# Layer 1 spline: the clip moved into scalar_tensor_tensor, r of every second half on VectorE, one distance instruction for a unit

## The chip, the cores and the metric

The kernel runs on one core of a Trainium2 chip. The metric is the device time of one launch in microseconds (us), the median of several runs. A core has five engines that run side by side: TensorE (PE, matmuls), VectorE (DVE, elementwise and reductions), ScalarE (ACT, functions of one input), GpSimd (POOL) and SyncE (SP, here the issue of DMA transfers). SBUF is the working memory of 128 partitions, PSUM the memory into which TensorE accumulates. Each engine takes its instructions in the order in which they were written down.

## The reference

The input x has 4 images of 16 channels and 256 x 256 pixels, float32. Two layers follow, each with a group normalization (8 groups) in front and the input added at the end:

```
x = x + L0(group_norm(x))     # a 3x3 convolution gives 25 weights a pixel and channel; softmax; weighted sum of the 5x5 patch
x = x + L1(group_norm(x))     # below
```

Layer 1 is the one that the change concerns. Its patches are 3 x 3 with padding 1:

```
bspl = b_splines(patches, grid)            # 8 cubic B-spline bases of every value, uniform grid
out  = silu(patches) . base_w  +  bspl . spl_w  +  bias
```

so that it is a 3x3 convolution over 16 x 8 spline features plus a 3x3 convolution over 16 silu features, to 16 output channels.

## The kernel before

**Layer 0** takes about the first two thirds. A chain of TensorE (logits), ScalarE (exponential), GpSimd (product) and VectorE (sum over the 25 places) runs over strips of columns. The change doesn't touch it. It writes its result x1 to DRAM.

**Layer 1** works on 64 units: 4 images, each in 16 bands of 16 rows. Its SBUF partitions are the 128 features: 16 channels x 8 spline bases. A loop over the units `n` writes down, for each:

- `features(n, put)`: the spline features of the 16 new rows of the unit, into `ring`, a buffer of 50 rows that holds three units and two rows more. The rows are worked in two halves of 8 rows (8 x 256 = 2048 elements a partition; at an image's first band one half has 9 rows, at its last 7). Between the halves, `put` (line 944) adds the bias to the finished output of the unit before the last and moves it from PSUM to SBUF.
- `silu(n, ...)`: the silu features of the unit (line 908), on ScalarE.
- `halo(n)`: zeroes at image borders; where the unit lies at the start of the ring, a DMA copies two rows from its end to its start.
- `load_x(n + 2)`: the loads of x1, two halves of 1 MB, each channel spread over eight partitions. There are three tiles, `xta`, `xtb` and `xtc`, used in turn (`xtt[n % 3]`).
- `store()` of an output, `load_tiles(n + 1)`: the tile `sx` for silu and the residual.
- `outputs(n, sx)`: 128 matmuls into `yp`: 96 on `ring` (line 961), 8 on `sx` (969), 24 on the silu features (977). All but the first two of the 96 need rows of half 1.

**The spline.** A basis is a function of the distance t of the normalized value from the basis' center, in grid steps. Up to a factor that the weights carry, it is

f = -max(2 - t, 0)^3 + 4 max(1 - t, 0)^3

For each half, ScalarE makes the distance in place in the tile of x1 (`Abs`, line 923), then r = max(1 - t, 0) (`Relu`, line 158), (2 - t)^2 into s2 (line 159) and 4 r^2 into s1 (line 160). VectorE clips t in place to min(t, 2) - 2 (line 161, a tensor_scalar), multiplies s2 by it (162) and s1 by r (163), and adds the two into `ring` (164). The temporaries r, s2 and s1 are one set for half 0 (`ta`) and one for half 1 (`tb`), with no second copy: ScalarE can fill a set for unit n+1 only when VectorE is done with it for unit n.

The order on each engine is the order of writing, for the loops above; a few units of layer 1 start while layer 0 ends, and their place among layer 0's instructions is given by marks. SyncE's issues also stand in this order: the loads of `n + 2` behind the ring copy of `n`, the sx tiles of `n + 1` behind the store of an output. `spline` is used once more at the start, for the value of the features outside the image (one element a partition).

Of the kernel before, what the change touches and what calls it, by code (L numbers as in the profile page):

```python
# [13 lines left out]
AF = mybir.ActivationFunctionType  # L14
ALU = mybir.AluOpType
# [18 lines left out]
def conv_preact_kernel(  # L34
# [12 lines left out]
    nc = tc.nc  # L47
    B, C, H, W = x.shape
# [34 lines left out]
    hs = [dram.tile([NST, HP, C, SP], F32, name=f"hs{b}") for b in range(B)]  # L83
# [68 lines left out]
        nc.gpsimd.tensor_tensor(rstd, var, mhalf, ALU.pow)  # L152
        return mean, rstd

    def spline(f, t, r1, s2, s1):


        nc.scalar.activation(r1, t, AF.Relu, bias=1.0, scale=-1.0)  # L158
        nc.scalar.activation(s2, t, AF.Square, bias=2.0, scale=-1.0)  # L159
        nc.scalar.activation(s1, r1, AF.Square, scale=2.0)  # L160
        nc.vector.tensor_scalar(t, t, 2.0, 2.0, ALU.min, ALU.subtract)  # L161
        nc.vector.tensor_mul(s2, s2, t)  # L162
        nc.vector.tensor_mul(s1, s1, r1)  # L163
        nc.vector.tensor_add(f, s2, s1)  # L164

    def scales(b, psum):

# [43 lines left out]
    sc = {}  # L211
# [177 lines left out]
    with tc.tile_pool(name="prep0", bufs=2) as prep, tc.tile_pool(  # L389
# [58 lines left out]
        nc.vector.tensor_copy(ub, ups)  # L448
        nc.scalar.activation(edge[:, 0:1], ub, AF.Abs)
        spline(*(edge[:, k : k + 1] for k in (4, 0, 1, 2, 3)))  # L450
        wps = pstat.tile([1, NL], F32, name="wps", tag="wps")

# [58 lines left out]
        for b in range(B):  # L511
            st = stat.tile([P, G, NH * (GC if b == 0 else 1), 6], F32, name=f"st0_{b}", tag=f"st0{min(b, 1)}")
            for hf in range(NH):
                n = b * NH + hf
                t = loaded.pop(0)
# [310 lines left out]
    def layer1(arm, last, marks):  # L826
# [3 lines left out]
        with ExitStack() as pools:  # L830
# [4 lines left out]
            def temps(name):  # L835
                p = pool(name)
                return [p.tile([P, RU // 2 + 1, W], F32, name=f"{name}{k}{arm}") for k in range(3)]

            def fixed(name, shape, n=1):
                p = pool(name)  # L840
                t = [p.tile(shape, F32, name=f"{name}{k}{arm}") for k in range(n)]
                return t

            XT = [P, RU + 1, W]
            xt0, tmp0 = fixed("xta", XT), temps("ta")
            sxp, yop = pool("sx", 2), pool("yo", 3)
            tmp1, xt1 = temps("tb"), fixed("xtb", XT)
            ring = fixed("ring", [P, 3 * RU + 2, W + 2])[0]
            sl, xtt = fixed("sl", [RD * C, RU // RT, W + 2], 2), xt0 + xt1 + fixed("xtc", XT)
# [13 lines left out]
            def halves(u):  # L863
                lo, hi = span(u)
                mid = (lo + hi + 1) // 2
                return lo, ((lo, mid), (mid, hi))
# [4 lines left out]
            def place(n):  # L871
                b, u = units[n]
                return (2 * (b % 2) + u) % 3 * RU
# [41 lines left out]
            def features(n, between):  # L915
                b, u = units[n]
                lo, hs = halves(u)
                r0 = place(n)
                for k, ((a, z), tmp) in enumerate(zip(hs, (tmp0, tmp1))):
                    if k == 1:  # L920
                        between()
                    xt = xtt[n % 3][:, a - lo : z - lo]
                    nc.scalar.activation(xt, xt, AF.Abs, scale=sc[b][2], bias=sc[b][3])  # L923
                    spline(
                        ring[:, r0 + a : r0 + z, 1 : W + 1], xt, *(t[:, 0 : z - a, :] for t in tmp)
                    )

            def halo(n):
                b, u = units[n]
# [70 lines left out]
            for t in sl:  # L1000
                for e in (0, W + 1):
                    nc.gpsimd.memset(t[:, :, e : e + 1], 0.0)
            features(0, put)
            first_silu = len(nc.cur_bb.bb.instructions)
            silu(0, sx[0])
            for n in range(len(units)):
                if n % 2:
                    next(more, None)
                if n > 0:
                    features(n, put)  # L1010
                    silu(n, sx[n])
                halo(n)
                if n + 2 < len(units):
                    for half in range(2):
                        load_x(n + 2, half)
                store()
                if n + 1 < len(units):
                    sx.append(load_tiles(n + 1))
                outputs(n, sx[n])
# [60 lines left out]
```

## Time and profile before

| what | value |
|---|---|
| time, median of 3 runs (lowest to highest) | 3223.17 us (3222.82 to 3223.66) |
| span of the profiled run | 3222.0 us |
| layer 1: first clip of unit 0 (L161) | starts at 2112.86 us |
| layer 1: first clip of unit 1 | starts at 2131.22 us |
| layer 1: last instruction on features (L164 of unit 63) | starts at 3199.07, takes 2.03 us |
| mean granted TensorE clock | 0.962 of full speed |

How to read the lines that follow: in the time lines, the columns are the start in us, the duration in us, the engine, the line of the kernel with operation, what is written and read, the shape (partitions x elements) and how many instructions were merged; in brackets stands how long the engine sat idle before and who released it. In the tables by stage, the columns are the stretch, its length, the busy time of PE, PEld (weight loads), DVE, ACT and POOL with instruction counts, the granted TensorE clock, the share of the DMA engines' time, and GB/s. Buffer numbers are left out of names.

### The profile page before, as it was taken

To read this page: it belongs to the slowest core of one execution; us is meant where nothing else is said; L and a number is where in the kernel's file an instruction comes from. 1 tells how busy PE (TensorE), PEld (TensorE's weight loads), DVE (VectorE), ACT (ScalarE), POOL (GpSimd) and SP (SyncE) were. 2 spreads that over 40 slices of the span, in tenths; PEclk is the share of its full clock that TensorE was granted. 3 is DMA by queue.
4 is the path that set the end of the run, shared out by engine and by line. 5 is a ranking of instruction groups with operands and counts; after the bars stand their busy time and mean duration, and the time that the engine had idled before them with its cause. 6 is when DMAs were issued, how large, how long until landed. Compare 5 with 4: busy or idle time off the path is not lost. (4 is left out here: it accounts for less than half of the span.)

```text
span 3222.0 us, 40428 instructions
## 1 busy us (share of the span) xinstructions
PE 2862.3 (89%) x14776; PEld 1490.7 (46%) x14776; DVE 3101.7 (96%) x1799; ACT 2208.0 (69%) x2233; POOL 1936.4 (60%) x659
## 2 busy tenths in 40 slices
PE   3499999999999999999999989859999989988988
PEld 3366665666566566656656656512222222222222
DVE  6589999999999999999999999999999999999997
ACT  6366555466554465554444444589999999999996
POOL 2299999999999999999999999900000000000000
PEclk7699999999999999999999999979999999999999
DMA  7988886778877788877756756678878778888883
GB/s 224 291 223 236 229 221 187 212 211 230 246 208 192 203 219 225 249 198 203 210 156 170 191 157 170 163 169 183 178 168 179 180 171 168 180 176 173 178 179 71
DMA packets 356531, 626.34 MB, mean 194 GB/s; under 512 B 45298, under 2 KB 222692, under 8 KB 340452
## 3 DMA queue, kind: packets, MB, share of 16 engines
q1 hardware_dynamic: 323300, 606.88, 75.3%
q10 hardware_dynamic: 33024, 16.78, 1.9%
q8 instruction: 121, 1.98, 0.3%
q14 instruction: 86, 0.70, 0.1%
HBM read 513.95 MB, written 104.24 MB: 192 GB/s over the span
## 5 line engine op out<-in xcount | busy, mean ns | idle before, releaser
L775 PE MATMUL lg<-wm,am 128*128 128x400 f32 x4096 | 1748.9, 508 | 123.4 <-ACT e L798 109.7
L803 POOL TENSOR_TENSOR e<-e,u 128x1600 f32<-128x1600 f32 x512 | 1789.1, 3536 | 68.5 <-ACT e L798 68.0
L680 DVE TENSOR_REDUCE nd<-e 128x128 f32<-128x3200 f32 x512 | 1747.5, 3477 | 23.3 <-POOL e L803 23.2
L798 ACT ACTIVATE e<-lg 128x800 f32<-128x800 f32 x1024 | 815.7, 836 | 896.5 <-DVE nd L680 768.9
L779 PE MATMUL lg<-wn,an 97*128 97x400 f32 x2048 | 1358.4, 663 | 0.5 <-DMA an<-hsl 0.5
L775 PEld LDWEIGHTS lg<-wm,am 128*128 128x128 f32 x4096 | 766.3, 194 | 450.1 <-ACT e L798 161.3
L961 PE MATMUL yp<-ring,wt 128*32 128x512 f32 x6144 | 755.1, 604 | 146.0 <-DVE ring L164 110.4
L779 PEld LDWEIGHTS lg<-wn,an 97*128 97x128 f32 x2048 | 390.8, 191 | 311.9 <-issue 15.6
L961 PEld LDWEIGHTS yp<-ring,wt 128*32 128x32 f32 x6144 | 206.5, 110 | 685.1 <-issue 477.9
L889 POOL MEMSET sx<- 16x256 f32 x8 | 2.4, 303 | 765.6 <-DMA out_dram<-yo 706.6
L977 PE MATMUL yp<-sl,ws 64*32 64x512 f32 x1536 | 176.5, 588 | 0.0
L164 DVE TENSOR_TENSOR ring<-ta,ta 128x2048 f32<-128x2048 f32 (+1 forms) x64 | 147.8, 2309 | 2.5
L164 DVE TENSOR_TENSOR ring<-tb,tb 128x2048 f32<-128x2048 f32 x64 | 145.6, 2276 | 2.6
L163 DVE TENSOR_TENSOR ta<-ta,ta 128x2048 f32<-128x2048 f32 (+1 forms) x64 | 147.3, 2301 | 0.0
L163 DVE TENSOR_TENSOR tb<-tb,tb 128x2048 f32<-128x2048 f32 x64 | 146.5, 2289 | 0.0
L908 ACT ACTIVATE sl<-sx,q 64x2048 f32<-64x2048 f32 x64 | 133.3, 2083 | 0.0
L160 ACT ACTIVATE ta<-ta 128x2048 f32<-128x2048 f32 (+1 forms) x64 | 122.3, 1911 | 0.0
L160 ACT ACTIVATE tb<-tb 128x2048 f32<-128x2048 f32 x64 | 120.5, 1883 | 0.6 <-POOL sx L889 0.6
L193 POOL TENSOR_TENSOR rstd<-rstd,mhalf 128x8 f32<-128x8 f32 x4 | 8.7, 2176 | 175.6 <-DVE rstd L191 175.6
L706 POOL TENSOR_TENSOR xc<-xc,nd 128x512 f32<-128x512 f32 x64 | 98.8, 1544 | 12.1 <-DVE nd L700 12.1
L977 PEld LDWEIGHTS yp<-sl,ws 64*32 64x32 f32 x1536 | 48.8, 106 | 116.2 <-issue 113.2
L923 ACT ACTIVATE xta<-xta,q 128x2048 f32<-128x2048 f32 (+2 forms) x44 | 91.6, 2083 | 0.0
(174 smaller groups left out, 2131.9 us busy)
## 6 DMA issues: line engine op xcount, KB each, us to landing
am<-hst SPq DMA_DIRECT2D x512, 194.6 KB
u<-hs SPq DMA_DIRECT2D x320, 288.0 KB
an<-hsl SPq DMA_DIRECT2D x512, 129.8 KB
xta<-x1s SPq DMA_DIRECT2D x40, 1024.0 KB
xtb<-x1s SPq DMA_DIRECT2D x40, 1024.0 KB
xtc<-x1s SPq DMA_DIRECT2D x40, 1024.0 KB
am<-hst SPq DMA_DIRECT2D x256, 129.8 KB
sx<-x1s SPq DMA_DIRECT2D x248, 128.0 KB
```

The source lines that it names most:

```text
L160: nc.scalar.activation(s1, r1, AF.Square, scale=2.0)
L163: nc.vector.tensor_mul(s1, s1, r1)
L164: nc.vector.tensor_add(f, s2, s1)
L680: nc.vector.tensor_reduce(nd[:, :, j : j + JG, :], e.rearrange("p t j m c d -> p t j c m d"), AX.XY, ALU.add,)
L706: nc.gpsimd.tensor_sub(v, v, nd[:, 1].rearrange("p j c -> p c j"))
L775: nc.tensor.matmul(lg[:, i, :NL], lhsT=am[:, o : o + P], rhs=wm.rearrange("p m c d -> p (m c d)"), start=True, stop=False,)
L779: nc.tensor.matmul(lg[:, i, :NL], lhsT=an[:, o : o + P], rhs=wn.rearrange("p m c d -> p (m c d)"), start=False, stop=True,)
L798: nc.scalar.activation(ev, lg[:, :, :NL], AF.Exp)
L803: nc.gpsimd.tensor_tensor(e[:, 1].rearrange("p j m c d -> p j (m c) d"), e[:, 0].rearrange("p j m c d -> p j (m c) d"), uv, ALU.mult,)
L908: nc.scalar.activation(sl[n % 2][:, :, 1 : W + 1], t, AF.Silu, scale=sc[b][0][0 : RD * C], bias=sc[b][1][0 : RD * C],)
L961: nc.tensor.matmul(yp[t * M : (t + 1) * M], lhsT=wt[:, d, e].rearrange("p r o -> p (r o)"), rhs=ring[:, r0 + t * RT + d : r0 + t * RT + d ...
L977: nc.tensor.matmul(yp[t * M : (t + 1) * M], lhsT=ws[:, e].rearrange("p r o -> p (r o)"), rhs=sl[n % 2][:, t : t + NT + 1 : NT, e : e + W], ...
```

## The change

Three edits to layer 1's features, meant to take work off ScalarE and VectorE:

1. **The clip goes into the two products.** Instead of min(t, 2) - 2 by an instruction of its own, s2 becomes (t - 2) (2 - t)^2 in one scalar_tensor_tensor. This is (t - 2)^3, negative inside the support and positive outside it. The last sum clips it: min(s2, 0) + s1, again one scalar_tensor_tensor.
2. **r of half 1 is made by VectorE.** `minus_r` computes min(t, 1) - 1 = -r in one tensor_scalar; with -r in place of r, s1 r comes out negative, and the last sum subtracts it. ScalarE's `Relu` remains for half 0 and for unit 0. minus_r is written ahead of both halves of its unit. Within a half, (2 - t)^2 now stands ahead of `Relu`.
3. **One distance instruction for a unit.** From unit 1 on, one `Abs` works on both halves (up to 4352 elements a partition) before anything else of the unit.

```diff
-    def spline(f, t, r1, s2, s1):
-        nc.scalar.activation(r1, t, AF.Relu, bias=1.0, scale=-1.0)
+    def minus_r(r1, t):
+        nc.vector.tensor_scalar(r1, t, 1.0, 1.0, ALU.min, ALU.subtract)
+
+    def spline(f, t, r1, s2, s1, given=False):
         nc.scalar.activation(s2, t, AF.Square, bias=2.0, scale=-1.0)
+        if not given:
+            nc.scalar.activation(r1, t, AF.Relu, bias=1.0, scale=-1.0)
         nc.scalar.activation(s1, r1, AF.Square, scale=2.0)
-        nc.vector.tensor_scalar(t, t, 2.0, 2.0, ALU.min, ALU.subtract)
-        nc.vector.tensor_mul(s2, s2, t)
+        nc.vector.scalar_tensor_tensor(s2, t, 2.0, s2, ALU.subtract, ALU.mult)
         nc.vector.tensor_mul(s1, s1, r1)
-        nc.vector.tensor_add(f, s2, s1)
+        nc.vector.scalar_tensor_tensor(
+            f, s2, 0.0, s1, ALU.min, ALU.subtract if given else ALU.add
+        )
...
-                for k, ((a, z), tmp) in enumerate(zip(hs, (tmp0, tmp1))):
+                parts = [
+                    (a, z, xtt[n % 3][:, a - lo : z - lo], [t[:, 0 : z - a, :] for t in tmp])
+                    for (a, z), tmp in zip(hs, (tmp0, tmp1))
+                ]
+
+                def distance(a, z):
+                    t = xtt[n % 3][:, a - lo : z - lo]
+                    nc.scalar.activation(t, t, AF.Abs, scale=sc[b][2], bias=sc[b][3])
+
+                if n > 0:
+                    distance(lo, hs[1][1])
+                    minus_r(parts[1][3][0], parts[1][2])
+                for k, (a, z, xt, tmp) in enumerate(parts):
+                    if n == 0:
+                        distance(a, z)
                     if k == 1:
                         between()
-                    xt = xtt[n % 3][:, a - lo : z - lo]
-                    nc.scalar.activation(xt, xt, AF.Abs, scale=sc[b][2], bias=sc[b][3])
-                    spline(
-                        ring[:, r0 + a : r0 + z, 1 : W + 1], xt, *(t[:, 0 : z - a, :] for t in tmp)
-                    )
+                    spline(ring[:, r0 + a : r0 + z, 1 : W + 1], xt, *tmp, given=n > 0 and k == 1)
```

## The prediction, made before the changed kernel ran

> **What bounds the kernel now.** I read the page's busy line first, then the busy table by stage, then the time lines of ScalarE, VectorE and TensorE through two units of layer 1, and last the DMA share unit by unit.
>
> ```profile
> PE 2862.3 (89%) x14776; PEld 1490.7 (46%) x14776; DVE 3101.7 (96%) x1799; ACT 2208.0 (69%) x2233; POOL 1936.4 (60%) x659
> ```
>
> This line would say VectorE, with ScalarE far from full. It is a mean over two layers. The changed lines run only in layer 1 (about 2110 us to the end), and there the table by stage gives, for 2300 to 3150 us, ACT 846.83 of 850 us and DVE 829.86. So both are nearly full, and the time line has to say which one waits. ScalarE through one unit, up to the start of the next:
>
> ```profile
> 2479.84 2.08 ACT L923 ACTIVATE xtb<-xtb,q 128x2048 f32<-128x2048 f32 x1
> 2481.95 1.91 ACT L158 ACTIVATE ta<-xtb 128x2048 f32<-128x2048 f32 x1
> 2483.77 1.89 ACT L159 ACTIVATE ta<-xtb 128x2048 f32<-128x2048 f32 x1
> 2485.57 1.90 ACT L160 ACTIVATE ta<-ta 128x2048 f32<-128x2048 f32 x1
> 2487.37 2.08 ACT L923 ACTIVATE xtb<-xtb,q 128x2048 f32<-128x2048 f32 x1
> 2489.48 1.91 ACT L158 ACTIVATE tb<-xtb 128x2048 f32<-128x2048 f32 x1
> 2491.30 1.90 ACT L159 ACTIVATE tb<-xtb 128x2048 f32<-128x2048 f32 x1
> 2493.10 1.90 ACT L160 ACTIVATE tb<-tb 128x2048 f32<-128x2048 f32 x1
> 2494.90 2.08 ACT L908 ACTIVATE sl<-sx,q 64x2048 f32<-64x2048 f32 x1
> 2496.89 2.08 ACT L923 ACTIVATE xtc<-xtc,q 128x2048 f32<-128x2048 f32 x1
> ```
>
> Nine instructions without a gap: 2496.89 - 2479.84 = 17.05 us a unit. VectorE, in the half unit that follows:
>
> ```profile
> 2502.75 1.23 DVE L161 TENSOR_SCALAR xtc<-xtc 128x2048 f32<-128x2048 f32 x1 [0.20 <-ACT ta L159]
> 2504.02 2.29 DVE L162 TENSOR_TENSOR ta<-ta,xtc 128x2048 f32<-128x2048 f32 x1
> 2506.22 2.29 DVE L163 TENSOR_TENSOR ta<-ta,ta 128x2048 f32<-128x2048 f32 x1
> 2508.55 2.29 DVE L164 TENSOR_TENSOR ring<-ta,ta 128x2048 f32<-128x2048 f32 x1
> 2510.76 0.74 DVE L944 TENSOR_SCALAR yo<-yp,bias_sb 128x512 f32<-128x512 f32 x1
> ```
>
> VectorE waits for ScalarE once a unit (0.2 to 0.3 us, up to 0.8). Left alone it needs 16.64 us: early in layer 1, where ScalarE is still ahead, the first multiplies of two units start at 2215.32 and 2231.96. So ScalarE's 17.05 us bounds, VectorE's 16.64 stands right behind it, and relieving ScalarE alone would bring 0.4 us a unit. TensorE waits for VectorE:
>
> ```profile
> 2536.59 10.51 PE L961 MATMUL yp<-ring,wt 128*32 128x512 f32 x94 [2.00 <-DVE ring L164]
> 2547.03 1.06 PE L969 MATMUL yp<-sx,wx 64*32 64x512 f32 x8
> 2547.91 2.76 PE L977 MATMUL yp<-sl,ws 64*32 64x512 f32 x24
> 2550.60 1.04 PE L961 MATMUL yp<-ring,wt 128*32 128x512 f32 x2
> ```
>
> From 2536.59 to 2550.60 is 14.01 us; two more matmuls cost some 0.2 of issue (94 take 10.51), so TensorE needs 14.2 us a unit. Some units have 12.2 instead of 10.5 us in the first row, nearly all behind a longer idle stretch. The DMA, in three windows of 17 us:
>
> ```profile
> 3017.00:3034.00 17.00, 14.99 (x136) 3.97 (x128) 16.54 (x10) 16.94 (x10) 0.00 (x0) 1.00 0.82 165
> 3034.00:3051.00 17.00, 14.99 (x135) 3.99 (x130) 16.54 (x10) 16.94 (x10) 0.00 (x0) 1.00 0.71 148
> 3051.00:3068.00 17.00, 15.00 (x132) 4.09 (x128) 16.54 (x10) 16.94 (x10) 0.00 (x0) 1.00 0.99 212
> ```
>
> The last two columns are the share of the DMA engines and GB/s. The mean, 175 GB/s x 17 us = 2.98 MB a unit, takes 14.0 us at the 212 GB/s seen at 0.99. It is the third resource that could take over.
>
> **What the Trainium skill says.** "VectorE: DVE Perf Modes", section "The perf-mode tier table", gives 2293 ns for a float32 tensor_tensor of 2048 elements in SBUF and 1227 for a tensor_scalar; the trace agrees (2.29 and 1.22). "ScalarE: Activation LUTs", section "What ACT_TABLE_LOAD costs", gives 0.833 ns an element and a fixed part, of which some 93 ns overlap the instruction before; here 2.08 us at 2048 and 2.29 to 2.30 at 2304 elements agree. "Vector Engine (DVE) Microarchitecture Reference", section "Points that are easy to get wrong", warns that scalar_tensor_tensor with two non-bf16 SBUF sources halves throughput, since no port is left to read the accumulator back. All four new instructions of a unit have two such sources. The trace has that operation only with one source in PSUM, beside a tensor_tensor of the same operands:
>
> ```profile
> 2091.69 0.69 DVE L699 SCALAR_TENSOR_TENSOR r<-nd,r 128x512 f32<-128x512 f32 x1
> 2092.42 0.69 DVE L700 TENSOR_TENSOR nd<-nd,r 128x512 f32<-128x512 f32 x1
> ```
>
> They are equal, so two operations in one instruction cost nothing there; two SBUF sources are not shown. No accumulator is used here, so I take the sentence as not applying, and keep it as a rival.
>
> **The change part by part, for one unit.** VectorE start to start, from the time line: an instruction that needs the one before it follows after its whole time and a little (2.31 us from L163 to L164), an independent one earlier (2.21 from L162 to L163).
>
> - Clip inside scalar_tensor_tensor: two L161 of 1.25 us go, 2.50 us. L162 and L164 stay one instruction each. Cost between 0 and +2048 cycles each, which is +2.1 us (the halved rate; one element a cycle is what 2.29 us for 2048 shows). I take +0.02, the start-to-start surplus of L699 over L698 (0.73 against 0.71).
> - minus_r: adds one tensor_scalar with the operation of L161: 1.22 us, 1.15 start to start as nothing after it needs it at once.
> - VectorE is then 1.15 + 2 x (2.21 + 2.31 + 2.21) + 0.66 (L944) + 4 x 0.02 = 15.35 us.
> - ScalarE: two Abs of 2.11 start to start become one of 4096 elements, 2.11 + 2048 x 0.833 ns = 3.82; one Relu goes. Relu now stands right before the Square that needs it (1.92 instead of 1.80, by the way Abs and its reader stand). Sum: 3.82 + 1.82 + 1.92 + 3 x 1.80 + 1.99 (Silu) = 14.95 us.
>
> The new wait: minus_r stands first in a unit on VectorE and waits for the whole unit's Abs; all of VectorE's unit is queued behind it. In turn the Square of 2r for half 1 waits for minus_r, and Silu and the next Abs are queued behind that on ScalarE. I count from the end of half 1's last sum in unit n-1 (0): ScalarE squares half 1 (freed at 0) to 1.9, 2r (minus_r done at 1.2) to 3.7, Silu to 5.7, Abs of n+1 to 9.5, half 0's three to 15.0; VectorE needs Abs at 15.35. The loop closes with 0.4 us over, and Abs is 5.9 us early. So both waits are hidden behind VectorE's own work.
>
> Loads: Abs now needs both halves of a unit's load. The time line of the DMA issues has xtc of one unit issued from 2465.78 on and first used at 2496.89, 31 us later; 2.1 MB need some 10 us. With both halves needed together and 15.35 us a unit, some 10 us stay over. The sx tiles are tighter: issued at 2462.98 behind TensorE, used by Silu at 2477.85; in the new order Silu comes about 19 us after TensorE's start on the unit before the last, the issue at 11.6 to 14, and the loads of xt stand ahead in the same queue: 2 to 3 us over.
>
> TensorE's 14.2 and the DMA's 14.0 us stay below 15.35, at 93% and 91%. VectorE becomes the bound.
>
> Sum: from VectorE's first instruction of unit 1 (2131.22) to its last of unit 63 (3201.10) are 1069.9 us, 16.98 for each of 63 units. New: 63 x 15.35 = 967.1, and 3.5 for the small VectorE instructions of the scales of images 2 and 3, which lie in this stretch. That saves 99.3. Unit 0 loses its two clips, 3 us, on VectorE behind the end of layer 0; ScalarE's Abs and Square of unit 1 (from 2121.5) follow in time. The tail after 3201.10 stays. 3223.2 - 99.3 - 3 = 3121 us. Layer 0 is untouched.
>
> **Rivals.**
> - The DMA sets the pace in part. For it: a unit of every three is at a share of 0.99, and transfers would have to fit into shorter units. Against it: nobody waits for a load from 2130 us on, and three units of loads may be under way. If every third unit stays at 16.9 us and the others fall to 15.35, the mean is 15.87: 63 x (16.98 - 15.87) = 70 saved, 3150 us. ScalarE's small margin or slow matmuls would end in the same stretch, up to a mean of 16.3, or 3177.
> - scalar_tensor_tensor at half rate: 15.35 + 4 x 2.13 = 23.9 us a unit, 63 x 23.9 + 3.5 = 1509 instead of 1070: about 3660 us, slower. For it: the skill's sentence. Against it: equal times at L699 and L700, and a reason that speaks of the accumulator.
> - The freed time is all taken up by TensorE or the load of sx and nothing is gained: 3223 us. Against it: TensorE's 2.0 us of idle in every unit.
>
> **How the numbers follow.** VectorE-bound 0.70, DMA or another partner in part 0.18, half rate 0.10, nothing gained 0.02. Predicted is the first, 3121. Its lower end: no surplus of scalar_tensor_tensor (63 x 0.08 = 5 us) and the last waits gone, 3110. The upper end takes in the second case to 3180; the half rate is left out with 1 in 10. Faster 0.87, same 0.02, slower 0.11.
>
> **What would show it.** Right: starts of minus_r 15.3 to 15.4 us apart with VectorE without gaps; ScalarE idle 0.3 to 0.5 us a unit before half 1's first Square; TensorE idle about 1.1 us; scalar_tensor_tensor at 2.29 us; one Abs of about 3.8 us; a DMA share of 0.9. Wrong: scalar_tensor_tensor near 4.4 us; or minus_r waiting for Abs with Abs or Silu waiting for a DMA.

## The result and the profile after

The changed kernel takes 3113.98 us (median of 4 runs, 3113.27 to 3114.57), the kernel before, run beside it, 3222.99: a ratio of 0.9662, 95% interval 0.9645 to 0.9678, or 109 us. The forecast was 3121 us, with a range of 3110 to 3180.

The busy line of the page of the changed kernel, and under it layer 1 from 2300 to 3050 us in the table by stage, of the kernel before and then of the changed one:

```profile
PE 2845.3 (91%) x14776; PEld 1494.9 (48%) x14776; DVE 3010.4 (97%) x1733; ACT 2083.5 (67%) x2107; POOL 1938.2 (62%) x659
```
```profile
2300.00:3050.00 750.00, 674.93 (x5646) 183.48 (x5642) 732.28 (x421) 747.21 (x397) 18.01 (x21) 0.98 0.82 174
2300.00:3050.00 750.00, 736.50 (x6282) 205.45 (x6278) 745.86 (x417) 736.15 (x345) 17.30 (x20) 1.00 0.92 195
```

The page's line hardly moves: VectorE 96 to 97%, ScalarE 69 to 67%. The stage tells more. VectorE is at 745.86 of 750 us, and from 2130 to 3100 us the trace has no wait of VectorE's over 0.15 us; ScalarE has come down from 747.21 to 736.15; the DMA share has gone from 0.82 to 0.92 because the same bytes move in less time. The bound has passed from ScalarE to VectorE. VectorE through one unit, up to the start of the next:

```profile
2465.19 1.22 DVE L156 TENSOR_SCALAR tb<-xtc 128x2048 f32<-128x2048 f32 x1
2466.33 2.28 DVE L165 SCALAR_TENSOR_TENSOR ta<-xtc,ta 128x2048 f32<-128x2048 f32 x1
2468.53 2.28 DVE L166 TENSOR_TENSOR ta<-ta,ta 128x2048 f32<-128x2048 f32 x1
2470.85 2.29 DVE L167 SCALAR_TENSOR_TENSOR ring<-ta,ta 128x2048 f32<-128x2048 f32 x1
2473.06 0.74 DVE L960 TENSOR_SCALAR yo<-yp,bias_sb 128x512 f32<-128x512 f32 x1
2473.72 2.28 DVE L165 SCALAR_TENSOR_TENSOR tb<-xtc,tb 128x2048 f32<-128x2048 f32 x1
2475.92 2.28 DVE L166 TENSOR_TENSOR tb<-tb,tb 128x2048 f32<-128x2048 f32 x1
2478.24 2.29 DVE L167 SCALAR_TENSOR_TENSOR ring<-tb,tb 128x2048 f32<-128x2048 f32 x1
2480.45 1.22 DVE L156 TENSOR_SCALAR tb<-xta 128x2048 f32<-128x2048 f32 x1
```

No line has a bracket with idle time. From minus_r (L156) to minus_r are 2480.45 - 2465.19 = 15.26 us. A scalar_tensor_tensor with two float32 sources in SBUF takes 2.28 or 2.29 us, as the tensor_tensor between does. ScalarE through the same unit:

```profile
2465.31 1.92 ACT L161 ACTIVATE tb<-xtc 128x2048 f32<-128x2048 f32 x1 [0.16 <-DVE ring L167]
2467.12 1.90 ACT L164 ACTIVATE tb<-tb 128x2048 f32<-128x2048 f32 x1
2468.92 2.08 ACT L913 ACTIVATE sl<-sx,q 64x2048 f32<-64x2048 f32 x1
2470.91 3.79 ACT L931 ACTIVATE xta<-xta,q 128x4096 f32<-128x4096 f32 x1
2474.73 1.91 ACT L161 ACTIVATE ta<-xta 128x2048 f32<-128x2048 f32 x1
2476.55 1.91 ACT L163 ACTIVATE ta<-xta 128x2048 f32<-128x2048 f32 x1
2478.49 1.91 ACT L164 ACTIVATE ta<-ta 128x2048 f32<-128x2048 f32 x1
2480.56 1.92 ACT L161 ACTIVATE tb<-xta 128x2048 f32<-128x2048 f32 x1 [0.16 <-DVE ring L167]
```

Here is the one wait that comes back, some 0.16 us in most units (45 waits from 2130 us on, 11.0 us in all): the Square of half 1 may overwrite its temporary only when VectorE's last sum has read it. The Abs of the next unit ends at 2474.70, 5.75 us before minus_r reads it, so the new wait of minus_r costs nothing. TensorE:

```profile
2464.09 1.04 PE L977 MATMUL yp<-ring,wt 128*32 128x512 f32 x2
2465.33 10.51 PE L977 MATMUL yp<-ring,wt 128*32 128x512 f32 x94 [0.20 <-DVE ring L167]
2475.77 1.06 PE L985 MATMUL yp<-sx,wx 64*32 64x512 f32 x8
2476.65 2.76 PE L993 MATMUL yp<-sl,ws 64*32 64x512 f32 x24
```

Its idle time ahead of the 94 matmuls has gone from 2.00 to 0.20 us. The sum over layer 1: VectorE's first instruction of unit 1 starts at 2127.80 (2131.22 before) and its last on features ends at 3090.97 (3201.10 before). Those 963.2 us were 1069.9 before.

### The profile page after: what moved, and what is told of

Same layout as the page of the kernel before. It is cut to its first block, busy times and chain, and to the rows that moved or that the text cites. A ratio compares the mean times of both kernels' runs of the same rounds, so it can differ in the third digit from the quotient of the medians.

```text
span 3112.0 us, 40438 instructions
## 1 busy us (share of the span) xinstructions
PE 2845.3 (91%) x14776; PEld 1494.9 (48%) x14776; DVE 3010.4 (97%) x1733; ACT 2083.5 (67%) x2107; POOL 1938.2 (62%) x659
## 4 chain that ended last, share of the span: by engine, by line
DVE 69%; PE 11%; ACT 6%; issue 6%; DMA 5%; SPq 2%; POOL 0%; DVEq 0%; ACTq 0%; POOLq 0%
DVE nd L685 48%; PE lg L780 5%; PE yp L977 4%; DVE ta L166 3%; DVE ta L165 3%; DVE tb L166 3%; DVE tb L165 3%; DVE ring L167 2%; DMA xin<-in_x_dram 2%; PE lg L784 1%; DVE st L719 1%; DVE tb L156 1%; DVE r L704 1%; DMA sx<-x1s 1%; DVE nd L703 1%
## 5 line engine op out<-in xcount | busy, mean ns | idle before, releaser
L977 PE MATMUL yp<-ring,wt 128*32 128x512 f32 x6144 | 737.9, 594 | 53.8 <-POOL ring L948 35.5
L167 DVE SCALAR_TENSOR_TENSOR ring<-ta,ta 128x2048 f32<-128x2048 f32 (+1 forms) x64 | 147.9, 2310 | 2.5
L167 DVE SCALAR_TENSOR_TENSOR ring<-tb,tb 128x2048 f32<-128x2048 f32 x64 | 145.7, 2276 | 2.6
L931 ACT ACTIVATE xta<-xta,q 128x4096 f32<-128x4096 f32 (+4 forms) x23 | 83.7, 3640 | 0.0
```

The lines of the kernel that those rows point to most:

```text
L167: nc.vector.scalar_tensor_tensor(f, s2, 0.0, s1, ALU.min, ALU.subtract if given else ALU.add)
L977: nc.tensor.matmul(yp[t * M : (t + 1) * M], lhsT=wt[:, d, e].rearrange("p r o -> p (r o)"), rhs=ring[:, r0 + t * RT + d : r0 + t * RT + d ...
```

## The experiments

**The three edits one at a time.** My theory was that a unit costs the larger of two sums, ScalarE's and VectorE's, each with the distances from start to start of the time line. The rival that the page suggests is that one engine's load alone counts.

*The clip alone* (e1):

```diff
-        nc.vector.tensor_scalar(t, t, 2.0, 2.0, ALU.min, ALU.subtract)
-        nc.vector.tensor_mul(s2, s2, t)
+        nc.vector.scalar_tensor_tensor(s2, t, 2.0, s2, ALU.subtract, ALU.mult)
...
-        nc.vector.tensor_add(f, s2, s1)
+        nc.vector.scalar_tensor_tensor(f, s2, 0.0, s1, ALU.min, ALU.add)
```

> The clip moved into the two scalar_tensor_tensor instructions, nothing else of the change. Theory (a unit costs the larger of ScalarE's and VectorE's own sums): ScalarE stays at 17.05 us a unit, VectorE falls from 16.64 to 14.1, so the pace stays; only the last unit, where VectorE runs behind ScalarE's last Square, ends some 3 us earlier: about 3220 us (3217 to 3223), with VectorE idle some 2.5 us more in every unit. Rival (VectorE's load is what the time follows, as its 96% on the page suggests): 63 x 2.5 us less, about 3066 us.

Measured: 3220.37 us beside 3222.52 of the kernel before, ratio 0.9992 (0.9985 to 0.9999). VectorE's time line shows where the 2.5 us a unit went (0.20 us idle at this place in the kernel before):

```profile
2723.21 2.29 DVE L161 SCALAR_TENSOR_TENSOR ta<-xta,ta 128x2048 f32<-128x2048 f32 x1 [2.70 <-ACT ta L159]
```

They became idle time in front of half 0, with ScalarE the one that VectorE waits for. On the engine that is not the bound, 15% less work is worth 2 us of 3222.

*minus_r alone* (e2): the clip instruction stays, half 1's last sum is a tensor_sub, and both halves' Abs stand ahead of minus_r. The edit is shown against the changed kernel, and shortened:

```diff
-        nc.vector.scalar_tensor_tensor(s2, t, 2.0, s2, ALU.subtract, ALU.mult)
+        nc.vector.tensor_scalar(t, t, 2.0, 2.0, ALU.min, ALU.subtract)
+        nc.vector.tensor_mul(s2, s2, t)
         nc.vector.tensor_mul(s1, s1, r1)
-        nc.vector.scalar_tensor_tensor(...)
+        (nc.vector.tensor_sub if given else nc.vector.tensor_add)(f, s2, s1)
...
-                    distance(lo, hs[1][1])
+                    for h in hs:
+                        distance(*h)
```

> minus_r for half 1 on VectorE, with the old clip instruction kept and two Abs ahead of the halves. Theory: ScalarE falls to some 15.1 us a unit, VectorE rises to 16.64 + 1.15 = 17.8, so slower: 63 x (17.8 - 16.98) = 52 us, about 3275 us. Rival (what paid was the Relu taken off ScalarE, the bound of before): 63 x 1.8 us less, about 3110 us.

Measured: 3274.60 us, ratio 1.0159 (1.0142 to 1.0176): slower by 52 us, as the theory has it. Now ScalarE is the one that waits:

```profile
2719.13 1.91 ACT L161 ACTIVATE tb<-xtb 128x2048 f32<-128x2048 f32 x1 [2.56 <-DVE ring L168]
```

*One Abs alone* (e3): the kernel before, with `distance(lo, hs[1][1])` ahead of both halves from unit 1 on.

> One Abs for a unit, nothing else of the change. Theory: ScalarE 17.05 - 0.40 = 16.65 us a unit, level with VectorE's 16.64, so 63 x 0.32 = 20 us less, about 3203 us (3200 to 3210). Rival (one Abs needs both halves' load and so waits for the DMA, or it delays half 0): 3223 us or more.

Measured: 3204.72 us, ratio 0.9943 (0.9927 to 0.9960). VectorE runs without a wait at 16.64 us a unit, and ScalarE waits for VectorE now and then (1.2 us in all from 2135 to 3080 us) and never for a load. Both sums are level, as reckoned, and one load for both halves holds nothing up.

*The clip and minus_r, without the one Abs* (e4): the changed kernel with the edit of `distance` shown under e2.

> The changed kernel with two Abs of one half each, both ahead of minus_r. Theory: ScalarE's 15.1 us stays just below VectorE's 15.26, so no difference: 3114 us, 3118 at most. Rival (ScalarE and VectorE wait for each other in turn, and ScalarE's margin is used up): 0.16 to 0.4 us a unit more, 3124 to 3139 us.

Measured: 3112.44 us (3111.88 to 3113.25), against 3113.98 for the change. The 1.5 us are not from this edit: its first instruction on features already starts at 2110.83 instead of 2112.32, at the end of layer 0, which is the same in both; from there to the last put are 992.5 and 992.9 us. So with the two other edits in place the third is worth nothing that can be measured.

Put together: -2, +52 and -18 us add up to +32, the three together give -109, and the first two without the third -110. The first two each use the room that the other makes: the clip frees 2.5 us on VectorE, of which minus_r takes 1.14, and the Relu that minus_r takes off ScalarE pays only once VectorE is shorter too. The order of Square and Relu within a half changed with the second edit, and no run has it alone; in ScalarE's lines of the changed kernel half 0's Square ends at 2476.64 us, and VectorE reads its result some 5 us later, so that an order with Square 1.8 us later would have held nothing up there (an estimate from these lines).

**The place of minus_r** (e5), the wait that the change adds. The edit against the changed kernel:

```diff
-                    minus_r(parts[1][3][0], parts[1][2])
...
                     if k == 1:
                         between()
+                        if n > 0:
+                            minus_r(tmp[0], xt)
```

> The changed kernel with minus_r written behind half 0 and put, just ahead of half 1. Theory: its place matters, since ScalarE's Square of 2r for half 1 waits for it, with Silu and the whole of the next unit's Abs and half 0 queued behind that wait; from one minus_r to the next runs 1.25 + 1.80 + 1.99 + 3.82 + 1.82 + 1.92 + 1.92 + 2.31 + 2.21 + 0.66 = 19.7 us through both engines, so about 3114 + 63 x 4.44 = 3394 us, with ScalarE idle some 4.7 us a unit before that Square. Rival (the sums of the engines alone set the pace, the order does not): 3114 us.

Measured: 3394.11 us beside 3224.78 of the kernel before, ratio 1.0525 (1.0507 to 1.0542). Same instructions, same sums, 280 us more than the changed kernel. VectorE and ScalarE around one unit's start:

```profile
2720.26 2.29 DVE L165 SCALAR_TENSOR_TENSOR ta<-xtb,ta 128x2048 f32<-128x2048 f32 x1 [2.59 <-ACT ta L161]
2724.01 2.29 DVE L166 TENSOR_TENSOR ta<-ta,ta 128x2048 f32<-128x2048 f32 x1 [1.45 <-ACT ta L164]
```
```profile
2710.91 1.91 ACT L164 ACTIVATE tb<-tb 128x2048 f32<-128x2048 f32 x1 [4.82 <-DVE tb L156]
2712.73 2.08 ACT L913 ACTIVATE sl<-sx,q 64x2048 f32<-64x2048 f32 x1
2714.71 3.57 ACT L931 ACTIVATE xtb<-xtb,q 128x3840 f32<-128x3840 f32 x1
```

ScalarE sits 4.82 us in front of the Square that needs -r, with Silu and the next Abs queued behind it; VectorE then waits for that Abs' readers. In this place of minus_r the larger of the two sums no longer sets the pace; where minus_r stands first in its unit, it does.

**Can the next engine be relieved as well?** In layer 1 GpSimd is nearly idle (17.30 of 750 us in the table by stage). e6 gives it one product a unit, so that VectorE can take r of both halves from ScalarE; e7 is the same with the product back on VectorE. Shortened to the lines that set the order:

```diff
+        minus_r(r0, ts[0])
+        minus_r(r1, ts[1])
+        for t, (r, s2, s1) in zip(ts, tmps):
+            nc.scalar.activation(s2, t, AF.Square, bias=2.0, scale=-1.0)
+            nc.scalar.activation(s1, r, AF.Square, scale=2.0)
+        nc.gpsimd.tensor_mul(s10, s10, r0)        # e7: nc.vector, behind between()
+        for t, (r, s2, s1) in zip(ts, tmps):
+            nc.vector.scalar_tensor_tensor(s2, t, 2.0, s2, ALU.subtract, ALU.mult)
+        between()
+        nc.vector.tensor_mul(s11, s11, r1)
+        for f, (r, s2, s1) in zip(fs, tmps):
+            nc.vector.scalar_tensor_tensor(f, s2, 0.0, s1, ALU.min, ALU.subtract)
```

> From unit 1 on, minus_r for both halves (no Relu on ScalarE), the product s1 r of half 0 on GpSimd, which is idle in layer 1, and VectorE's order: both minus_r, both (t-2)^3, put, product of half 1, the two last sums. Theory: VectorE 2.35 + 6 x 2.2 - 2.2 + 0.66 + 0.1 = 14.1 us a unit, ScalarE 13.1, TensorE 14.2 and DMA 14.0 to 14.3; the pace becomes 14.3 to 14.6, that is 3054 to 3072 us. Rival A (GpSimd and VectorE disturb each other, so that VectorE's instructions of 2.29 us grow or GpSimd's product takes far more than 4.5 us): no faster than 3114. Rival B (the DMA, at a share of 0.92 now, cannot go faster): 3100 us or more, with ScalarE waiting for loads.

> As e6_gpsimd_product, but the product of half 0 stays on VectorE: the same order and the same work, less the move to GpSimd. Theory: VectorE 15.26 + 1.14 = 16.4 us a unit, so 3114 + 63 x 1.14 = 3186 us. Rival (VectorE has slack left by the rest): 3114 us.

Measured: e6 3311.21 us, ratio 1.0267 (1.0250 to 1.0284); e7 3204.13 us, ratio 0.9937 (0.9921 to 0.9954). My theory for e6 falls, and its rival A has it. VectorE and GpSimd in e6:

```profile
2721.37 2.28 DVE L180 SCALAR_TENSOR_TENSOR ta<-xta,ta 128x2048 f32<-128x2048 f32 x1
2724.17 6.10 DVE L180 SCALAR_TENSOR_TENSOR tb<-xta,tb 128x2048 f32<-128x2048 f32 x1 [0.51 <-ACT tb L176]
```
```profile
2722.40 5.72 POOL L178 TENSOR_TENSOR ta<-ta,ta 128x2048 f32<-128x2048 f32 x1 [7.83 <-ACT ta L177]
```

GpSimd's product is recorded from 2722.40 on, while VectorE's first instruction runs to 2723.65. From there to its end at 2728.12 are 4.47 us, and layer 0's rate on GpSimd (3.536 us for 1600 elements) gives 4.53 for 2048. VectorE's second instruction is recorded from 2724.17 and ends at 2730.27, 2.15 us behind GpSimd's end, not quite its own 2.28. Each behaves as if it stood still while the other ran. The Trainium skill states this in "SBUF — State Buffer", section "SBUF: two separate sides": a GpSimd instruction that reads SBUF and a VectorE instruction with two SBUF inputs share a pair of ports by an exclusive lock, and the one that comes second blocks. The trace agrees: VectorE gave away a product of 2.2 us, and its instruction beside GpSimd's grew by 3.84 (6.13 us on average, 2.29 in e7). That is a loss of 1.64 us a unit, or 103 us of the 107 between e6 and e7. Rival B was not put to the test: a unit took 18.36 us, and ScalarE never waited for a load.

e7 misses by 18 us for a reason of its own. VectorE is at 16.68 us a unit instead of 16.4:

```profile
2715.17 2.28 DVE L179 SCALAR_TENSOR_TENSOR ta<-xta,ta 128x2048 f32<-128x2048 f32 x1
2717.90 2.29 DVE L179 SCALAR_TENSOR_TENSOR tb<-xta,tb 128x2048 f32<-128x2048 f32 x1 [0.45 <-ACT tb L176]
```

With r of half 0 made by VectorE too, ScalarE's Square of half 1 stands behind a Square that waits for minus_r, and comes 0.45 us late. My sum had no chain through both engines in it. Without that wait a unit would be at 16.23 us, 0.2 less than reckoned: in the new order no VectorE instruction follows at once on the one whose result it needs, and two steps of 2.32 us become 2.20.

**What is left on VectorE.** If its own sum is the whole pace, even 0.1 us of it must show. e8 puts the bias instruction where it fills the delay behind a needed result; e9 does the same in half 1 with the next unit's minus_r. Shortened to the place of the call:

```diff
         nc.vector.tensor_mul(s1, s1, r1)
+        between()               # e8: put, in half 0; e9 also: Abs and minus_r of unit n + 1, in half 1
         nc.vector.scalar_tensor_tensor(
             f, s2, 0.0, s1, ALU.min, ALU.subtract if given else ALU.add
         )
```

> The changed kernel with put written between the product and the last sum of half 0, so that the last sum no longer follows at once on the product that it needs. Theory (VectorE's own sum is the whole pace, 2.31 us behind a needed result and 2.21 otherwise): 15.26 - 0.1 = 15.16 us a unit, 3114 - 6 = 3108 us. Rival (ScalarE, TensorE or the DMA already share in the pace): 3113 to 3115 us.

> As e8_put_between, and from unit 1 on the next unit's Abs and minus_r written ahead of the last sum of half 1, which takes the second such step away. Theory: 15.06 us a unit, 3102 us; ScalarE's 14.95 is then nearly level. Rival (ScalarE's margin is used up, or minus_r must wait as long behind the product that reads the old r): 3108 us or more.

> The changed kernel itself, on the same chip as the two others: 3114 us.

Measured, on one chip: e8 3106.07 us (3104.29 to 3107.04), e9 3110.62 (3110.00 to 3110.99), the changed kernel 3113.54 (3112.27 to 3114.66). Against the kernel before (3222.03 on this chip), e8 is at 0.9639 (0.9626 to 0.9652). VectorE in e8:

```profile
2708.57 2.29 DVE L166 TENSOR_TENSOR ta<-ta,ta 128x2048 f32<-128x2048 f32 x1
2710.77 0.75 DVE L962 TENSOR_SCALAR yo<-yp,bias_sb 128x512 f32<-128x512 f32 x1
2711.43 2.28 DVE L168 SCALAR_TENSOR_TENSOR ring<-ta,ta 128x2048 f32<-128x2048 f32 x1
```

The product is now followed after 2.20 us instead of 2.32, and a unit takes 15.13 us (minus_r starts at 2705.23 and 2720.36). e8 beats both kernels, by 7.5 us against the changed one. In e9:

```profile
2718.76 2.29 DVE L166 TENSOR_TENSOR tb<-tb,tb 128x2048 f32<-128x2048 f32 x1
2721.14 1.23 DVE L156 TENSOR_SCALAR tb<-xtb 128x2048 f32<-128x2048 f32 x1
2722.28 2.28 DVE L168 SCALAR_TENSOR_TENSOR ring<-tb,tb 128x2048 f32<-128x2048 f32 x1
```

minus_r overwrites the r that the product has just read, and follows after 2.38 us: the delay is not filled but moved, and a little longer. A unit takes 15.19 us, not 15.06, so the 3102 us expected of e9 fail by 8.6, and the second half of its rival has it. The first half doesn't: VectorE has no wait over 0.15 us for ScalarE in e9.

## Why the prediction was right

**ScalarE bounded before, with VectorE right behind.** Shown by e1 and e3: VectorE's work alone is worth nothing (-2 us), ScalarE's alone 18 us, until VectorE's 16.64 us stop it.

**scalar_tensor_tensor at full rate.** Right, and the heaviest of the open questions: 2.28 us with both sources in SBUF. The Trainium skill's sentence on halved throughput ("Vector Engine (DVE) Microarchitecture Reference", section "Points that are easy to get wrong") does not hold for this use, without an accumulator; a use with one was not run. Of my four surcharges of 0.02 us nothing is there; this is the term of the sum that was too large, 63 x 0.08 = 5 us of the 7 by which the forecast was too high. The rest is 1.4 us in the scales' small instructions (963.2 - 63 x 15.255 leaves 2.1, I had 3.5) and a fraction at the start: unit 1 begins 3.4 us earlier, I had 3, and 0.5 of the 3.4 come from layer 0, whose end differs by that much between the two traces.

**VectorE 15.35 us a unit.** 15.26 measured. minus_r costs 1.14 us start to start (I had 1.15).

**ScalarE 14.95 us.** 15.09 by its starts (15.25 from Square to Square of half 1, less 0.16 idle): the Square of half 1 waits for VectorE's last sum. Without a wait it would start 1.80 us after the Square of 1.91 us before it, so about 0.1 us before that one's end, and this overlap is lost too. So ScalarE's idle time is 0.16 us, not 0.3 to 0.5. It stayed hidden, and e4, with still less room (Abs of 3.97 instead of 3.82), shows that it did not matter.

**The new wait of minus_r is hidden because it stands first.** Abs ended 5.75 us ahead of it (5.9 reckoned), and e5 shows what another place costs: 19.7 us a unit by the same way of counting (19.74 measured on average), and 3394 us to the microsecond.

**TensorE's idle time of about 1.1 us.** Wrong as put: 0.2. The row of two matmuls ahead of the wait is shown as 1.04 us, where two of the 94 take some 0.2 (an estimate from 10.51 us for 94); I took 14.2 from 15.3, but the trace counts the whole 1.04 as busy. The idle time shown fell by just what a unit became shorter, 2.00 - 1.80.

**The DMA.** A share of 0.92 against 0.91 reckoned. The sx tiles, reckoned at 2 to 3 us over, were late once: in unit 1 Silu waited 0.28 us for them. But the DMA did not set the pace, since e8 went to 15.13 us a unit and 197 GB/s and still followed VectorE's sum. Where it would begin to, no run here shows.

## What to carry to other kernels

When two engines run level through a loop, take each one's sum over one turn from start to start, find what the change does to both, and take the larger: edits that are worth -2 and +52 us alone were worth -110 together. Then follow each wait that the change adds once around through both queues, for the same instructions in another place cost 280 us more. And try whether an idle engine is room: GpSimd's product and VectorE's instruction took turns in e6, and the move cost 107 us.

## What was not expected of the hardware

- GpSimd and VectorE took turns in e6: 6.13 us instead of 2.29 for VectorE's instruction, 5.72 with some 1.2 of standing still for GpSimd's. The page of the Trainium skill named under e6 has this case; I gave it too little weight in the expectation.
- In e9 the VectorE instruction that overwrites what the one before it reads follows as late as one that reads its result: 2.38 us behind a 2.29 us product in e9, 2.32 in the ordinary order, 2.20 when independent.
- Of the 57 rows of 94 matmuls that stand alone in the kernel before, nine took about 12.2 instead of 10.5 us. The prediction read nearly all of them as standing behind a longer idle stretch. In fact five do (2.6 to 6.1 us), and four stand behind 1.9 to 2.1 us, as much as the usual 2.0. In the changed kernel, where TensorE's idle time is mostly 0.2 to 1.2 us, only the row of the first unit is slow (12.56 us), and the mean granted clock from 2300 to 3050 us is 1.00 instead of 0.98. Idle time alone doesn't decide it: in the kernel before most rows behind 2.0 us of it ran at 10.5, while in e1, at the same 2.0 us, 31 of 54 rows took 11.95 to 12.51, at a clock of 0.95 in that stretch. A unit of e1 took 17.05 us all the same, so the slow matmuls cost nothing there. What decides it stays open.
